# Loading and transposing the columns of the edge products in the relational stage, and comparing fp32 columns into one-hots

## The chip, the cores and the metric

One Trainium2 chip, one core. The metric is the device time of one launch in microseconds (us). The profile is of one execution of the program. Its engines are PE (TensorE matmuls, with PEld for its weight loads), DVE (VectorE), ACT (ScalarE), POOL (GpSimd) and SP (SyncE, which here only issues DMAs; "SPq" in the trace). Each engine works off its own queue in order and waits at semaphores for the others.

## The reference, cut to what matters

A graph network of four layers over 3125 nodes with 256 features each; every layer is a graph part and a feed-forward part, each added to x. There are 53125 edges (src, dst), sorted by dst. What bears on the change:

- layer 1, graph part ("relational"): `agg = segment_sum(hx[edge_type, src], dst)`, where hx holds x times the weight of each of 8 relations
- layer 1, feed-forward part: a mixture of 4 experts, whose gates come from an attention layer over a second list of edges ("the gates")
- layer 2, graph part: two graph convolutions, `segment_sum((h @ W)[src] * norm, dst)`, over the same edges as the relational part

The kernel computes the sums of layer 2 as products with an adjacency matrix in bf16, whose blocks are made in advance. The change is in how these blocks are made.

## The kernel before, in words

Nodes are sorted by degree and cut into 25 groups of 128 (NT = 25); group g has KS[g] edge slots per node (41 for the first, 10 for the last, 453 in all). X, the nodes' rows, stays in SBUF.

**Adjacency blocks.** `edge_places` (L1746) computes for every edge slot the source's partition and a block number and writes both to slots_d in DRAM (L1762, 25 DMAs on SP, at 1692.7 us). `edge_columns` (L1764) reads them back: it fills W ("em_w", 128 x 5 x 2 x 128 fp32) with 512.0 on DVE, loads it with 45 DMAs on SP (L1774, L1777), and makes `columns` ("em_c"), the numbers 0 to 255, by an iota on POOL. The function it returns, `turn` (L1784), transposes W in ten 128x128 transposes on PE into PSUM, from which ACT copies it to `cols` ("em_cols"). `one_hots` (L1793) then compares cols with columns for one group: two tensor_tensor instructions on DVE, into "em_p" (who is the source) and "em_b" (which block). `edge_blocks` (L1804) multiplies the two on PE ("em_ps"), and ACT copies the products to "em_a", which goes to adj in DRAM.

**The relational stage** (from L2253). `plain_sum` (L1690) gathers, slot by slot, 453 tiles of 128 rows from rel with indirect DMAs issued by POOL (L1079), and PE sums them (L1705). `pipeline` (L1088) writes the order of the gathers, sums and tails out by hand (`tc.manual_schedule`) while there are gathers left. Beside it, four steps a turn, runs `route_merge` (L1870), which sorts the second list of edges, mostly on DVE; its first DMA on SP is the load of rm_c (L1890), which PE's L1897 waits for. It uses a PSUM tile m_ps with a single buffer. The tails write gm, the table that the gates gather from.

**The gates** (`gates_by_slots`, L2307) lie inside a `tc.If`. `in_turns` (L1575) writes the order out by hand: turn by turn, for each group, POOL gathers the list (recs, L2327), the node's own row (own, L2329) and 428 tiles from gm (L2334), DVE scores and sums them (L2337 to L2357). Beside it, some pieces a turn, runs `beside_gates` (L2413): 28 units of the experts' hidden layers (L2438, L2452) on PE, and at i = 2 `turn`, from i = 3 on the one-hots of group i - 3, from i = 4 on the products of group i - 4. The first turn takes four pieces, later ones one or two. Once the gates are there, X takes up the experts' rows, which SP loads as y (L2518).

**What is not written out by hand** is put in order by a planner: it takes instructions when it thinks that their inputs and memory are ready, and may place them ahead of others traced earlier. Memory is given out pool by pool; a pool that is opened where another was closed waits for that one's tiles.

Of the kernel before, what the change touches and what calls it, by code (L numbers as in the profile page):

```python
# [11 lines left out]
F32 = mybir.dt.float32  # L12
BF16 = mybir.dt.bfloat16
# [7 lines left out]
P = 128  # L21
# [3 lines left out]
NT = (N + P - 1) // P  # L25
# [1388 lines left out]
def quick(ctx: ExitStack, tc: tile.TileContext, a: dict, out: bass.AP, k):  # L1414
# [3 lines left out]
    nc, dram, ident, ones = tc.nc, k.dram, k.ident, k.ones  # L1418
# [304 lines left out]
    TB = -(-at // P)  # L1723
# [37 lines left out]
            o = slice(OFF[g], OFF[g] + KS[g])  # L1761
            nc.sync.dma_start(slots_of(g).rearrange("(s p k) -> p s k", s=2, p=P), pb[:, :, o])  # L1762

    def edge_columns(wp, psum):  # L1764


        W = wp.tile([P, TB, 2, P], F32, name="em_w")
        nc.vector.memset(W, 512.0)
        for g, (w, n, at) in enumerate(TILES):
            e = w * KS[g]  # L1770
            full, rest = P // w, P % w * KS[g]
            rows = slots_of(g).rearrange("(s m) -> s m", s=2)
            r = at % P
            nc.sync.dma_start(W[r : r + full, at // P, :, :e],  # L1774
                              rows[:, : full * e].rearrange("s (i e) -> i s e", e=e))
            if rest:
                nc.sync.dma_start(W[r + full : r + n, at // P, :, :rest],  # L1777
                                  rows[:, full * e :].rearrange("s (i e) -> i s e", i=1))
        columns = wp.tile([P, 256], BF16, name="em_c")
        nc.gpsimd.iota(columns, pattern=[[1, 256]], base=0, channel_multiplier=0,  # L1780
                       allow_small_or_imprecise_dtypes=True)
        cols = wp.tile([P, TB, 2, P], BF16, name="em_cols")

        def turn():  # L1784
            for b in range(TB):
                ps = psum.tile([P, 2, 256], F32, name="em_ps", bufs=3)
                for s in range(2):
                    nc.tensor.transpose(ps[:, s, :P], W[:, b, s, :], ident)
                nc.scalar.copy(cols[:, b, :, :], ps[:, :, :P])

        return cols, columns, turn

    def one_hots(pool, cols, columns, g):  # L1793
        w, n, at = TILES[g]
        e, z = w * KS[g], w * NT
        part = pool.tile([e, n, P], BF16, name="em_p")
        block = pool.tile([e, n, z], BF16, name="em_b")
        m = slice(at % P, at % P + n)
        for t, s, c in ((part, 0, P), (block, 1, z)):
            nc.vector.tensor_tensor(t, columns[:e, None, :c].to_broadcast([e, n, c]),  # L1800
                                    cols[:e, at // P, s, m][:, :, None].to_broadcast([e, n, c]), ALU.is_equal)
        return part, block
# [182 lines left out]
    with tc.tile_pool(name="gg", bufs=gbufs) as gp, tc.tile_pool(name="gm", bufs=3) as mp, \  # L1985
# [78 lines left out]
        for _ in lists:  # L2064
            pass

    with tc.tile_pool(name="rt", bufs=1) as rt_pool:
        pieces, G = route_pieces(rt_pool)

# [6 lines left out]
        with tc.tile_pool(name="sc", bufs=1) as sc:  # L2076
# [24 lines left out]
            with tc.tile_pool(name="tkp", bufs=1, space=PSUM) as tkp, tc.tile_pool(name="sk", bufs=2) as sk:  # L2101
# [4 lines left out]
                for c0, n in CHUNKS:  # L2106
                    xmt = sk.tile([P, PP, 512], F32, name="xmt")
                    for c in range(PP):
                        ps = tkp.tile([P, 512], F32, name="xm_ps", bufs=2)
# [42 lines left out]
            with tc.tile_pool(name="atp", bufs=1, space=PSUM) as atp, tc.tile_pool(name="sb", bufs=1) as sb:  # L2152
# [18 lines left out]
                for w, nm in ((wq, "qt"), (wk, "kt")):  # L2171
                    ps = atp.tile([P, PP, P], F32, name="a_ps", bufs=3)
# [80 lines left out]
        with tc.tile_pool(name="rg", bufs=12) as gp, tc.tile_pool(name="rs", bufs=2) as sp, \  # L2253
                tc.tile_pool(name="rc", bufs=1) as wp, tc.tile_pool(name="rcp", bufs=1, space=PSUM) as psum:
            wl = f.kxn(a["L1_gnn_loop_weight"], D, wp, "w_loop")
            hb = f.row(a["L1_gnn_h_bias"], D, wp, "h_bias")
            wg = f.kxn(a["L1_ffn_W_gat"], HC, wp, "wg")
            at_r = wp.tile([P, 2, HC], F32, name="at_r")
            for i, n in enumerate(("att_src", "att_dst")):
                ap = a["L1_ffn_" + n]  # L2260
                nc.sync.dma_start(at_r[:, i, :], bass.AP(tensor=ap.tensor, offset=ap.offset, ap=[[0, P], [1, HC]]))

            def loop(acc, g):
                for c in range(KD):
                    nc.tensor.matmul(acc, XNT[:, c, g * P : (g + 1) * P], wl[:, c, :], start=(c == 0), stop=False)

            def tail(g, acc):
                nc.vector.scalar_tensor_tensor(X[:, g, :], acc, 0.5 ** 0.5, X[:, g, :], op0=ALU.mult, op1=ALU.add)
                nc.vector.tensor_add(X[:, g, :], X[:, g, :], hb)
                if g % BATCH < BATCH - 1:  # L2270
                    return
                yield 0
                gs = range(g - BATCH + 1, g + 1)
                yield from norm_pieces(sp, psum, gs)
                tbs = []
                for g_ in gs:
                    ps = psum.tile([P, HC], F32, name="hg_ps", bufs=2)
                    f.node_matmul(ps, g_, wg, slice(0, HC))
                    tb = sp.tile([P, GW], F32, name="tb", bufs=2 * BATCH)
                    tv = tb[:, : H * (C + 1)].rearrange("p (h c) -> p h c", h=H)  # L2280
                    nc.vector.memset(tb, 1.0)
                    nc.vector.tensor_copy(tb.bitcast(I32)[:, H * (C + 3) : H * (C + 3) + 1], place[:, g_ : g_ + 1])
                    nc.scalar.copy(tv[:, :, :C], ps.rearrange("p (h c) -> p h c", h=H))
                    m = sp.tile([P, 2, HC], F32, name="m2")
                    nc.vector.tensor_mul(m, ps[:, None, :].to_broadcast([P, 2, HC]), at_r)
                    nc.vector.tensor_reduce(tb[:, H * (C + 1) : H * (C + 3)],
                                            m.rearrange("p s (h c) -> p (s h) c", h=H), AX.X, ALU.add)
                    tbs.append(tb)
                    yield 0
                yield 0  # L2290
                yield 0
                for g_, tb in zip(gs, tbs):
                    scatter(tc, "gm", gm, pid(g_), tb)
                    yield 0

            merge = route_merge(wp, lambda n: psum.tile([P, P], F32, name="m_ps")[:, :n], pieces, G)
            plain_sum(rel, relz, gp, psum, loop, tail, merge)
            for _ in merge:
                pass


    gd = dram.tile([NP, C], F32, name="gd")
# [110 lines left out]
    def beside_gates(pool, wp, psum):  # L2413
# [6 lines left out]
        ws, hts, os_, ys, hots, As = {}, {}, {}, {}, {}, {}  # L2420
# [43 lines left out]
            nc.sync.dma_start(each_d[e, c0 : c0 + n, :].rearrange("(i p) d -> p i d", p=P), ys.pop(u)[:, : n // P, :])  # L2464

        load(0)
        cols, columns, turn = edge_columns(wp, psum)
        clear = itertools.chain(cleared(sw_in), cleared(top_in))
        U = len(units)
        for i in range(U + 3):  # L2470
            if i % len(CHUNKS) == 2 and i // len(CHUNKS) + 1 < EX:
                load(i // len(CHUNKS) + 1)
            if 0 <= i - 2 < U:
                biased(i - 2)
            if i == 2:
                turn()
            if 3 <= i < NT + 3:
                hots[i - 3] = one_hots(pool, cols, columns, i - 3)
            g = i - 4
            products = iter(())  # L2480
            if 0 <= g < NT:
                As[g] = pool.tile([P, NT, P], BF16, name="em_a")
                products = edge_blocks(psum, g, *hots.pop(g), As[g])
            work = [hidden(i)] if i < U else []
            if 0 <= i - 1 < U:
                work.append(back(i - 1))
            for _ in itertools.chain(*work):
                next(products, None)
            for _ in products:
                pass  # L2490
            if 0 <= i - 3 < U:
                store(i - 3)
            if 0 <= g - 1 < NT:
                nc.sync.dma_start(adj[g - 1], As.pop(g - 1).rearrange("p b j -> p (b j)"))
            next(clear, None)
            yield 0
# [9 lines left out]
    with c2.Else():  # L2506
        with tc.tile_pool(name="gc", bufs=1) as gc:
            gates_by_tiles(gc)
        with tc.tile_pool(name="gc", bufs=1) as gc, tc.tile_pool(name="gx", bufs=2) as xp, \
                tc.tile_pool(name="gxp", bufs=1, space=PSUM) as psum:  # L2510
            for _ in beside_gates(xp, gc, psum):
                pass
    with tc.tile_pool(name="ge", bufs=1) as gc, tc.tile_pool(name="gy", bufs=4) as gp:
        gates = gc.tile([P, NT, C], F32, name="gates")
        nc.sync.dma_start(gates, gd.rearrange("(p t) w -> p t w", p=P))
        for g in range(NT):
            y = gp.tile([P, 4, D], F32, name="y")
            nc.sync.dma_start(y, each_d[:, g * P : (g + 1) * P, :].rearrange("e p d -> p e d"))  # L2518
            for e in range(4):
                nc.vector.scalar_tensor_tensor(X[:, g, :], y[:, e, :], gates[:, g, e : e + 1], X[:, g, :],  # L2520
                                               op0=ALU.mult, op1=ALU.add)
# [476 lines left out]
```

## Time and profile before

| what | us |
|---|---|
| median of 5 runs | 5851.42 |
| lowest and highest run | 5832.91, 5855.75 |
| the profiled execution | 5851.66 |
| its span, from the first to the last instruction | 5849.7 |
| PE busy | 3840.9 (66%) |
| DVE busy | 3125.5 (53%) |
| ACT busy | 1220.0 (21%) |
| POOL busy | 3167.3 (54%) |
| relational stage, in the span | 2102 to 2771 |
| gates, in the span | 2771 to 3513 |
| comparisons L1800, 25 into em_p and 25 into em_b | 69.6 and 89.2 on DVE |

A row of the profile's groups has: line, engine, operation, output and inputs by the program's names, count; busy time in us and the mean of one in ns; the idle time of the engine ahead of them, and what ended it. A line in order of time has: start in the span, duration, engine, line, operation, and in brackets the idle time ahead of it with what ended it ("issue" where it waited for nothing that the profile shows). The table by stage has for each engine the busy time and the number of instructions, then the granted TensorE clock, the share of the DMA engines and their rate.

### The profile page before, as it was taken

The numbers are of one execution on the slowest core, as the hardware profiler recorded it, in microseconds if no ns is written. First come the engines' busy times: TensorE is split into PE (matmuls) and PEld (weight loads), VectorE is DVE, ScalarE is ACT, GpSimd is POOL, SyncE is SP. The second block draws the span as 40 slices with busy tenths as digits, with TensorE's granted clock in tenths as the row PEclk, the third lists the DMA queues.
The fourth block names the chain that finished last, engine by engine and source line by source line (L and its number), as shares of the span: only waits on it lengthen the run. The fifth ranks groups of instructions, "written<-read, shape, count | busy, mean of one in ns | idle before, by whom it ended". The sixth has DMA issues, their size and how long they took to land. (4 is left out here: it accounts for less than half of the span.)

```text
span 5849.7 us, 45124 instructions
## 1 busy us (share of the span) xinstructions
PE 3840.9 (66%) x14119; PEld 2472.2 (42%) x14119; DVE 3125.5 (53%) x6023; ACT 1220.0 (21%) x2574; POOL 3167.3 (54%) x3044
## 2 busy tenths in 40 slices
PE   2345544355578978676866602989587999658882
PEld 1234333233455534344544401556343555446661
DVE  4588877999975356611444416332226889700001
ACT  1222222445642200000333301110021000012220
POOL 4577774777776057777777773010106777520005
PEclk9676766667789976666988856999656878779996
DMA  4533343333321233323532214332243333334442
GB/s 123 147 105 108 107 109 87 100 97 102 108 51 46 111 101 105 101 73 88 152 109 64 67 31 146 105 106 96 75 129 94 102 99 100 104 124 158 151 158 83
DMA packets 357952, 602.93 MB, mean 103 GB/s; under 512 B 109331, under 2 KB 254331, under 8 KB 354370
## 3 DMA queue, kind: packets, MB, share of 16 engines
q0 software_dynamic: 130800, 329.16, 20.9%
q1 hardware_dynamic: 207657, 251.79, 13.4%
q10 hardware_dynamic: 19238, 18.93, 1.0%
q8 instruction: 115, 1.88, 0.1%
q14 instruction: 142, 1.16, 0.1%
HBM read 458.77 MB, written 142.93 MB: 103 GB/s over the span
## 5 line engine op out<-in xcount | busy, mean ns | idle before, releaser
L1620 PE MATMUL acc<-wv,ident 128*128 128x256 f32 x2818 | 906.6, 481 | 574.4 <-ACT wv L1632 296.2
L1079 POOL DMA_INDIRECT gt<-T,recs x906 | 1005.1, 1109 | 307.9 <-issue 219.6
L1620 PEld LDWEIGHTS acc<-wv,ident 128*128 128x128 f32 x2818 | 652.4, 242 | 828.6 <-ACT wv L1632 343.9
L1079 POOL DMA_INDIRECT gt<-gm,recs x428 | 511.4, 1195 | 138.9 <-issue 115.5
L1079 POOL DMA_INDIRECT gt<-TA,recs x453 | 469.4, 1036 | 139.4 <-issue 122.8
L1079 POOL DMA_INDIRECT gt<-rel,relz x453 | 441.3, 974 | 141.8 <-issue 121.5
L1705 PE MATMUL acc<-gt,ident 128*128 128x256 f32 x906 | 419.2, 577 | 144.0 <-DMA gt<-rel,relz 136.9
L2566 PE MATMUL acc<-XNT,adj_g 128*128 128x512 bf16 x1250 | 416.2, 384 | 47.0 <-ACT XNT L2558 47.0
L1672 ACT ACTIVATE m<-m 128x1024 f32<-128x1024 f32 (+2 forms) x258 | 256.5, 994 | 625.5 <-DVE m L1671 625.2
L1079 POOL DMA_INDIRECT y<-top_out,top_pos x50 | 47.8, 957 | 596.9 <-issue 595.7
L1671 DVE TENSOR_TENSOR m<-gt,R 128x1028 f32<-128x1028 f32 (+4 forms) x258 | 297.4, 1153 | 117.9 <-DMA gt<-T,recs 114.5
L1705 PEld LDWEIGHTS acc<-gt,ident 128*128 128x128 f32 x906 | 202.8, 264 | 342.8 <-DMA gt<-rel,relz 330.6
L2569 PE MATMUL acc<-F,adj_g 128*128 128x256 bf16 x1250 | 342.9, 275 | 5.7 <-DVE F L2559 5.7
L2438 PE MATMUL x_ps<-XNT,x_w 128*128 128x512 f32 (+1 forms) x448 | 214.8, 613 | 172.1 <-ACT x_h L2440 161.9
L2797 PE MATMUL e_ps<-EW,att 32*128 32x512 f32 (+7 forms) x466 | 289.7, 747 | 49.8 <-ACT att L2787 33.7
L2909 PE MATMUL fh_ps<-xt,w 128*128 128x256 f32 x1024 | 266.9, 399 | 76.2 <-ACT ht L2911 75.4
L1677 DVE TENSOR_TENSOR m<-m,att 128x1024 f32<-128x1024 f32 (+2 forms) x258 | 294.2, 1140 | 27.8 <-ACT m L1672 27.8
L1678 DVE TENSOR_REDUCE L<-m 128x4 f32<-128x1024 f32 (+4 forms) x258 | 294.3, 1141 | 8.0
L1634 DVE TENSOR_TENSOR wv<-gt,L 128x1024 f32<-128x1024 f32 (+3 forms) x252 | 285.3, 1137 | 0.9 <-PE acc L1620 0.8
L2909 PEld LDWEIGHTS fh_ps<-xt,w 128*128 128x128 f32 x1024 | 187.7, 193 | 150.3 <-ACT ht L2911 128.1
L2901 DVE COPY xt<-ft_ps 128x512 f32<-128x512 f32 x32 | 22.1, 692 | 388.9 <-PE ft_ps L2900 388.9
L1083 POOL DMA_INDIRECT gcn<-own,PR x50 | 64.6, 1291 | 304.4 <-ACT ht L1455 228.5
(557 smaller groups left out, 6748.4 us busy)
## 6 DMA issues: line engine op xcount, KB each, us to landing
w<-in_L_ffn_W_dram SPq DMA_DIRECT2D x64, 1024.0 KB
adj_g<-adj SPq DMA_DIRECT2D x50, 800.0 KB
adj<-em_a SPq DMA_DIRECT2D x25, 800.0 KB
gt<-T,recs POOLq DMA_INDIRECT x906, 2.8
y<-each_d SPq DMA_DIRECT2D x25, 512.0 KB
each_d<-x_y SPq DMA_DIRECT2D x24, 512.0 KB
R<-rr SPq DMA_DIRECT2D x25, 388.0 KB
top_in<-zeros SPq DMA_DIRECT2D x8, 1024.0 KB
```

The source lines that it names most:

```text
L1079: return nc.gpsimd.indirect_dma_start(out=out_, out_offset=None, in_=table, in_offset=index(idx))
L1620: nc.tensor.matmul(acc, ident, wv[:, s, :], start=(c + s == 0), stop=(c + s == K - 1))
L1634: nc.vector.tensor_mul(wv[:, :n, :].rearrange("p s (h c) -> p s h c", h=H), t[:, :n, :D].rearrange("p s (h c) -> p s h c", h=H), L[:, c : ...
L1671: nc.vector.tensor_add(m[:, :n, :], st[g].tiles[c][:, :n, :], st[g].R[:, 1:2, :].to_broadcast([P, n, W]))
L1672: nc.scalar.activation(m[:, :n, :D], m[:, :n, :D], AF.Abs)
L1677: nc.vector.tensor_mul(m[:, :n, :D], m[:, :n, :D], att[:, None, :].to_broadcast([P, n, D]))
L1678: nc.vector.tensor_reduce(L, m[:, :n, :D].rearrange("p s (h c) -> p s h c", h=H), AX.X, ALU.add)
L1705: nc.tensor.matmul(accs[g], ident, t[:, s, :], start=False, stop=(last and s == n - 1))
L2566: nc.tensor.matmul(acc.rearrange("p s d -> p (s d)"), A[:, b, :], F12[:, b, :, :].rearrange("p s d -> p (s d)"), start=(b == 0), stop=Fals ...
L2569: nc.tensor.matmul(acc[:, 0, :], A[:, b, :], F3_[:, b, :], start=False, stop=(b == NT - 1), skip_group_check=True)
L2797: nc.tensor.matmul(e_ps[:, :z, :].rearrange("p s d -> p (s d)"), att, EW[: att.shape[0], s0 : s0 + z, :].rearrange("p s d -> p (s d)"), st ...
L2909: nc.tensor.matmul(ps[:, i, :], ld[j][1][:, c, (f_ + i) * P : (f_ + i + 1) * P], xt[j][:, c, :], start=(c == 0), stop=(c == KD - 1))
```

## The change

`edge_columns` takes a pool for W, and is called before `plain_sum` in the relational stage instead of at the start of `beside_gates`. The call hands eq over as wp: columns and cols lie in the new pool "eq", which is opened ahead of the slice attention (`held`) and closed after the gates; W lies in the pool that is handed over as `pool`, the relational stage's own. `turn` is called after the merge, at the end of the relational stage, goes through the m_ps tile one transpose at a time, and makes ten copies instead of five. columns and cols are fp32 instead of bf16, so that both inputs of the comparisons in `one_hots` are fp32; their outputs remain bf16. In `beside_gates` the one-hots of group i are made at i, and the products of group i - 1 at i: three pieces earlier than before.

```diff
-    def edge_columns(wp, psum):
+    def edge_columns(wp, pool):
-        W = wp.tile([P, TB, 2, P], F32, name="em_w")
+        W = pool.tile([P, TB, 2, P], F32, name="em_w")
         nc.vector.memset(W, 512.0)
...
-        columns = wp.tile([P, 256], BF16, name="em_c")
+        columns = wp.tile([P, 256], F32, name="em_c")
         nc.gpsimd.iota(columns, pattern=[[1, 256]], base=0, channel_multiplier=0,
                        allow_small_or_imprecise_dtypes=True)
-        cols = wp.tile([P, TB, 2, P], BF16, name="em_cols")
-
-        def turn():
+        cols = wp.tile([P, TB, 2, P], F32, name="em_cols")
+
+        def turn(psum):
             for b in range(TB):
-                ps = psum.tile([P, 2, 256], F32, name="em_ps", bufs=3)
                 for s in range(2):
-                    nc.tensor.transpose(ps[:, s, :P], W[:, b, s, :], ident)
-                nc.scalar.copy(cols[:, b, :, :], ps[:, :, :P])
+                    ps = psum.tile([P, P], F32, name="m_ps")
+                    nc.tensor.transpose(ps, W[:, b, s, :], ident)
+                    nc.scalar.copy(cols[:, b, s, :], ps)
...
+    held = ExitStack()
+    eq = held.enter_context(tc.tile_pool(name="eq", bufs=1))
     with tc.tile_pool(name="rt", bufs=1) as rt_pool:
...
+            cols, columns, turn = edge_columns(eq, wp)
             merge = route_merge(wp, lambda n: psum.tile([P, P], F32, name="m_ps")[:, :n], pieces, G)
             plain_sum(rel, relz, gp, psum, loop, tail, merge)
             for _ in merge:
                 pass
+            turn(psum)
...
         load(0)
-        cols, columns, turn = edge_columns(wp, psum)
...
-            if i == 2:
-                turn()
-            if 3 <= i < NT + 3:
-                hots[i - 3] = one_hots(pool, cols, columns, i - 3)
-            g = i - 4
+            if i < NT:
+                hots[i] = one_hots(pool, cols, columns, i)
+            g = i - 1
...
+    held.close()
```

## The prediction

> **What bounds the kernel now.** I read the slices of the span first, then the groups, then the order in time around the places that the diff touches. The change lies in two stages: the relational one (2102 to 2771 us of the span) and the gates (2771 to 3513). The table by stage shows neither PE nor DVE full there:
>
> ```profile
> core 0: us, PE busy (x) PEld busy (x) DVE busy (x) ACT busy (x) POOL busy (x), PEclk, DMA share, GB/s
> 2102.00:2771.00 669.00, 477.76 (x1164) 264.29 (x1164) 302.43 (x723) 14.59 (x55) 504.53 (x543) 0.65 0.34 91
> 2771.00:3513.00 742.00, 434.58 (x1751) 279.69 (x1751) 283.77 (x492) 224.95 (x476) 581.63 (x501) 0.79 0.32 85
> ```
>
> POOL is the bound of both. In the gates it has 501 instructions, 0.30 us pass between two of them ("issue"), and 581.6 + 501 x 0.30 = 732 of the 742 us. So what the change is worth is what it does to POOL's queue. Of that queue one row is too dear:
>
> ```profile
> L1079 POOL DMA_INDIRECT gt<-gm,recs x428 | 511.4, 1195 | 138.9 <-issue 115.5
> ```
>
> Undisturbed such a gather takes 0.94 us. Laid beside DVE in order of time, it is seen what stretches the others:
>
> ```profile
> 2817.20 5.88 DVE L1800 TENSOR_TENSOR em_p<-em_c,em_cols 123x5504 bf16<-123x5504 bf16 x1
> 2818.00 5.90 POOL L1079 DMA_INDIRECT gt<-gm,recs  x1 [0.98 <-DMA gt<-gm,recs]
> 2823.00 3.52 DVE L1800 TENSOR_TENSOR em_b<-em_c,em_cols 123x3225 bf16<-123x3225 bf16 x1
> 2824.21 3.12 POOL L1079 DMA_INDIRECT gt<-gm,recs  x1 [0.30 <-issue]
> ```
>
> The first gather ends at 2823.90, 0.82 us after em_p ends (2823.08); the second at 2827.33, 0.81 after em_b. I went through the whole stage: of the 51 gathers that start under an L1800, 50 are stretched, and the mean of the 51 is 3.08 us. That is 51 x (3.08 - 0.94) = 109 us of POOL's time. The question of the change is therefore whether an fp32 comparison holds POOL for less.
>
> **fp32 comparisons.** The same two views in the relational stage answer it. L1926 is a tensor_tensor of fp32 with both inputs in SBUF:
>
> ```profile
> 2134.99 2.29 DVE L1926 TENSOR_TENSOR rp_g<-rp_g,rm_t 125x2048 f32<-125x2048 f32 x1
> 2136.09 2.02 POOL L1079 DMA_INDIRECT gt<-rel,relz  x1 [0.30 <-issue]
> ```
>
> This gather ends at 2138.11, 0.83 after the fp32 instruction: held in the same way. So are gathers under L1671, L1677 and L1634 of the attention layers (f32, 45 stretched in 300 us, nearly all ending 0.81 to 0.84 us after it). And the length: an em_p of 128x2048 bf16 takes 2.30 us, L1926 with 2048 fp32 elements 2.29, L1924 with int32 against f32 2.29. Fp32 inputs with a bf16 output are not in the trace; the nearest rows bound the difference by 0.02 us either way, x 50 instructions = -1 to +1 us. I take 0, as the rows are equal.
>
> The Trainium skill speaks against this edit: "VectorE: DVE Perf Modes", section "The perf-mode tier table", gives tensor_tensor twice the rate on bf16 in SBUF that it has on fp32. By that the 158.8 us of comparisons would double, and an estimate from that page is up to 159 us more on POOL, some 6010 us. This trace disagrees: its bf16 comparisons run at the fp32 rate already, and one of their inputs is broadcast along the inner axis, where the page asks for a step of one. On the hold, the skill's "SBUF - State Buffer", section "Who interferes with whom", infers that a tensor_tensor doesn't starve the making of descriptors; the 50 rows above differ, and the measurement decides.
>
> **The columns leave the gates.** What goes, one by one. On POOL the iota em_c (0.37 us, 0.28 before the next): it stands between the gather of own and the first of gt, on the path: -0.65. On DVE the memset (1.12 us): DVE then idles 27.8 us until PE's first output, 0. On PE 10 transposes (1.55 us) and on ACT 5 copies (1.55): neither is the bound, 0. On SP 45 loads, 2774.2 to 2799.9, 25.7 us; queued behind them are zeros for sw_in and the second expert's weights, issued at 2801 and used an expert later: 0.
>
> **Where they go.** columns and cols lie in the new pool eq, W in the relational stage's own pool, whose memory comes free at 2102 us. So the 45 loads can't be moved into SP's idle time before (it issues nothing from 1849.3 to 2102.3); only the em_c iota can. The start of the stage, in order of time:
>
> ```profile
> 2102.29 0.37 SPq L57 DMA_DIRECT2D w_loop<-n_L_gnn_loop_weight_dram  x1
> ...
> 2104.68 0.43 SPq L1890 DMA_DIRECT2D rm_c<-route_n  x1
> 2110.70 0.42 PE L1897 MATMUL m_ps<-rm_c,ones 128*128 128x2 f32 x2
> 2112.94 0.15 DVE L1900 COPY rm_b<-m_ps 128x2 f32<-128x2 f32 x1
> 2113.20 2.81 DVE L1909 TENSOR_SCALAR rm_t<-rp_g 125x2048 int32<-125x2048 int32 x1
> ...
> 2118.77 2.29 DVE L1914 TENSOR_TENSOR rm_t<-rm_t,rm_u 125x2048 int32<-125x2048 int32 x1
> 2130.36 2.28 POOL L1915 IOTA rm_u<- 125x2048 int32 x1
> 2132.67 2.29 DVE L1924 TENSOR_TENSOR rm_t<-rm_u,rm_n 125x2048 f32<-125x2048 int32 x1 [6.88 <-POOL rm_u L1915]
> ```
>
> The reader is to see a chain: rm_c, a small sum on PE, four passes on DVE, then POOL's second iota into rm_u, which must wait until L1914 has read the first. It has 9.3 us of slack (2121.06 to 2130.36).
>
> W's memset and loads are traced ahead of plain_sum, and rm_c stands inside the order written by hand, behind them. What the planner did with work of that kind: the zero rows of rel (L2073), traced after two attention layers, go out at 184.7 us; the iota of place (L2252) stands at 1669.5, ahead of 128 gathers traced before it. It goes by readiness, then by traced order. The loads are ready once the memset is done (1.1 us after 2102), so I put them ahead of rm_c. Then, step by step: five other loads as now, 45 loads by the 25.7 us that they took in the gates, rm_c issued at 2104.7 + 25.7 = 2130.4. A small load of this place lands some 2.5 us after its issue (h_bias issued at 2102.71, first read on PE at 2105.2), so L1897 runs at about 2133 and L1900 at 2133.5. It then takes L1909 (2.81, of which 1.6 look like POOL's first iota beside it: the like L1912 takes 1.23), L1910 1.29, L1912 1.23, L1914 2.29: it ends between 2140.0 and 2141.5. POOL waits from 2130.4 to there: 9.6 to 11.1 us more. Two gathers that now run before the iota, undisturbed, come to lie under these passes: about 1.8 us. Together 11.4 to 12.9, and I take the middle: **+12.2 us**.
>
> What of the rest of the 20 us by which DVE is late? DVE waits 34.8 us for POOL's rm_base (L1953, 2487.7) and 8.5 for rm_all (L1933): there the merge catches up. PE's sums start late by as much, but 12 chunk buffers lie between, and POOL nowhere waits for PE beyond its 0.30. Nothing further is late: 0. What would speak against it is in the third rival. On POOL the iota em_c, hoisted, falls among early gathers with idle time behind them (21 us before 2069.7): 0.
>
> **The transposes.** Ten rounds through a single m_ps buffer: transpose, copy, transpose. The nearest row is the norm's round (two transposes and a copy of 128x256), 1.17 us a round at the end of this stage, so at most 12 us on PE and ACT. m_ps is free from 2627, when the merge ends. PE idles 191 us of this stage and is buffered by 12 chunks; ACT works 15 us of 669. Put last instead, the rounds fall into PE's wait of 10.2 us for the first weights (2767.3 to 2777.5): at worst 2 us, on PE, which isn't the bound. I take 0.
>
> **One-hots and products three pieces earlier.** The same 25 pairs, still within POOL's gathers, hold POOL as long as before: 0 (-1 to +1 for how they meet the gathers). New is that the first turn holds four pairs instead of one. Could DVE then be late for POOL? The gathers of group 4 need the tile that group 0's sum frees: that sum ends at 2874, they start at 2958.9, 85 us of margin. PE's extra is three products of about 3.0 us (74.5/25), less the 1.55 of transposes. 0.
>
> **Sum.** The profiled execution took 5851.66 us (span 5849.7 and 2.0 around it). 5851.66 - 0.65 + 12.2 = 5863.2; the median of the runs, 5851.42, lies 0.2 lower. I forecast 5863. Its own range takes POOL's wait and the stretched gathers from below and above, with 3 to 5 us for what the steps at nothing may bring: 5858 to 5871.
>
> **Rivals.**
> 1. *Not slower: rm_c goes ahead of the loads.* If the planner or the hand-written order takes rm_c first, or the loads are spread between the steps of the merge, the chain stands as it is and only the iota's 0.65 is left: 5851. It decides while rm_c is issued before about 2119 (L1914 ends 9.6 to 11.1 us after rm_c's issue in the steps above, and POOL wants it read at 2130.4). For it: readiness alone (rm_c needs nothing but memory, the loads a memset first). Against it: rm_c is traced inside the hand-ordered part, behind the loads.
> 2. *Faster: rm_c ahead, and transfers around the gates earlier.* POOL's waits in the gates beyond 0.30 us add up to some 10.8 us (2.07, 0.81, 4.04, 1.04, 1.34 and smaller), mostly for lists whose transfers are late; without 45 loads ahead of them they might go, and the loads of y (1.84 us each) start one sooner in eq's memory. 5851.0 - 10.8 - 1.8 = 5838. Against it: the bulk transfers of weights remain, only 25.7 us sooner.
> 3. *Slower by the whole delay.* rm_c is late by 25.7 us, of which 19.6 to 20.6 reach L1914; if the later waits of POOL for the merge grow too (5.1 us for L1217 at 2509.7 is one), POOL loses all of it: 5851 + 20 = 5871. Against it: the 34.8 us that DVE waits for POOL shortly before.
> 4. *fp32 does release POOL.* Then 109 us go: 5742 without a delay. Against it stand the L1926 rows.
> 5. *fp32 costs DVE more.* Each per cent of the 158.8 us holds POOL 1.6 us longer: ten per cent and the delay make 5879. Against it: the equal lengths.
>
> **How the numbers follow.** Forecast 62%, first rival 20, second 8, third 8, fourth 1, fifth 1. The bound of 0.2% is 11.7 us here (about what a measurement of this kernel can tell from no change), so slower begins at 5863.1, in the middle of the forecast's own range; of its 13 us, 8 lie above, so I count 37 of its 62 as slower and 25 as the same. Slower: 37 + 8 + 1 = 46%. The same: 25 + 20 = 45%. Faster: 8 + 1 = 9%. The range takes in the forecast and the first three rivals at their prices, and leaves out the last two: 5838 to 5872.
>
> **What would show it.** Right: em_w's loads on SP from about 2104 to 2130 and rm_c behind them; POOL waiting ahead of rm_u's second iota until about 2140; no iota of em_c in the gates; L1800's groups with f32 inputs at the lengths of now (2.3 us for 128x2048) and gathers of gm at a mean near 1195 ns. Wrong: rm_c near 2105 (first and second rival), a longer wait of POOL near 2510 (third), a mean of gm near 0.95 us (fourth), longer L1800 (fifth), or a wait of POOL for DVE early in the gates, which would say that the 85 us of margin were not there.

## The result, and the profile after

The changed kernel takes 5847.81 us (median of 34 runs, 5831.29 to 5865.35), the kernel before 5851.07 (58 runs): a ratio of 0.9996, 95% interval 0.9990 to 1.0002. That is no change. The profiled execution of the changed kernel took 5851.69 us, with a span of 5849.9, the same as before.

A difference of nothing hides two stages that moved by 8 us and more. First the relational stage, in order of time, after the change:

```profile
2125.46 1.82 POOL L2737 MEMSET EW<- 32x2048 f32 x1
2128.39 0.35 SPq L1890 DMA_DIRECT2D rm_c<-route_n  x1
2135.35 2.29 DVE L1914 TENSOR_TENSOR rm_t<-rm_t,rm_u 125x2048 int32<-125x2048 int32 x1
2137.71 3.22 POOL L1915 IOTA rm_u<- 125x2048 int32 x1 [10.43 <-DVE rm_t L1914]
```

The 45 loads of em_w stand on SP from 2104.55 to 2128.28, rm_c behind them: 23.7 us later than before. L1914 ends at 2137.64 instead of 2121.06, and POOL, which before reached its second iota with no wait, now idles 10.43 us ahead of it. One line is new here, and no part of the diff speaks of it: EW, the table of edge weights of the last layer, is filled on POOL at 2125. It is not alone: the five other loads of its pool on SP (w, bias, wg, bg, a_row), issued from 3408.7 on before, now go out right behind rm_c, from 2128.8 on.

The other place is the end of the gates. Before the change (first fence) EW's fill and its 16 loads on SP stood between the last scatter of the gates and the load of `gates`; after it (second fence) they are gone from there:

```profile
3532.32 0.96 POOL L1083 DMA_INDIRECT gd<-gates_o,own_at  x1 [0.30 <-issue]
3533.28 1.82 POOL L2735 MEMSET EW<- 32x2048 f32 x1
...
3540.26 0.35 SPq L2515 DMA_DIRECT2D gates<-gd  x1
```

```profile
3537.03 0.97 POOL L1083 DMA_INDIRECT gd<-gates_o,own_at  x1 [0.30 <-issue]
3539.21 0.34 SPq L2517 DMA_DIRECT2D gates<-gd  x1
```

From the start of the last scatter to the load of `gates` it was 7.9 us and is 2.2.

I followed POOL's gathers one by one through both traces, and noted how much later each starts after the change. The list is the account of the whole result:

| place | later than before by, us |
|---|---|
| gather 20 of rel (2140.9 before) | 9.3 |
| last gather of rel | 8.1 |
| first gather of gm | 8.2 |
| gather 20 of gm | 23.6 |
| gather 200 of gm | 15.5 |
| last gather of gm | 4.7 |
| load of `gates` | -1.1 |
| end of the last sum of the experts' rows into X | 2.2 |
| span | 0.2 |

The first row adds up from single differences: the first gather +0.65; gathers ahead of the iota, which no longer lie under the merge's passes, -5.5; EW's fill +1.8; the wait +10.4; the iota, now beside a pass of DVE, +0.9; gathers after it +1.0. A later wait of POOL for DVE (L1217) became 1.2 us shorter. In the gates the four pairs of comparisons of the first turn now hold the first gathers (+15.4 by gather 20), and later gathers are freed in return, until the gates have taken 3.5 us less than before (737.2 to 733.7 from the first gather to the last): 2.2 of them on the gathers of lists, one of which lay under a comparison before, and 1.1 on those of gm. The last 5.7 are EW. Behind the load of `gates` that gain doesn't stay whole: the 25 loads of y take 48.0 us from the first to the last where they took 45.6, so the last sum into X ends 2.2 us later than before. Why they take longer isn't known. From there to the end the changed kernel is 2.0 us quicker, which is little beside the 34 us over which the runs of one kernel are spread.

The comparisons themselves have not changed. This is the last one into em_p, before (first fence) and after:

```profile
3359.50 1.88 DVE L1800 TENSOR_TENSOR em_p<-em_c,em_cols 100x1664 bf16<-100x1664 bf16 x1
```

```profile
3307.24 1.88 DVE L1800 TENSOR_TENSOR em_p<-em_c,em_cols 100x1664 bf16<-100x1664 f32 x1
```

The group of gathers from gm takes 510.3 us (511.4 before), and under the comparisons 50 gathers are still stretched:

```profile
L1079 POOL DMA_INDIRECT gt<-gm,recs x428 | 510.3, 1192 | 139.0 <-issue 116.7
```

### The profile page after: what moved, and what is told of

It reads as the page before. It is cut to its first block, busy times and chain, and to the rows that moved or that the text cites. A ratio compares the mean times of both kernels' runs of the same rounds, so it can differ in the third digit from the quotient of the medians.

```text
span 5849.9 us, 45128 instructions
## 1 busy us (share of the span) xinstructions
PE 3839.9 (66%) x14119; PEld 2475.5 (42%) x14119; DVE 3125.7 (53%) x6023; ACT 1221.6 (21%) x2579; POOL 3156.5 (54%) x3044
## 5 line engine op out<-in xcount | busy, mean ns | idle before, releaser
L1079 POOL DMA_INDIRECT gt<-gm,recs x428 | 510.3, 1192 | 139.0 <-issue 116.7
L2923 PE MATMUL fo_ps<-w,ht 128*128 128x256 f32 x1024 | 226.3, 379 | 0.0
```

Source lines behind the costliest of these rows:

```text
L1079: return nc.gpsimd.indirect_dma_start(out=out_, out_offset=None, in_=table, in_offset=index(idx))
L2923: nc.tensor.matmul(ps[:, i, :], h[:, f_, i * P : (i + 1) * P], w2[:, f_, :], start=(f_ == 0), stop=(f_ == FC3 - 1))
```

## The experiments

Theory T, formed from the account above: the edits act through POOL's queue; the late rm_c costs 8 to 9 us, EW's new place brings nearly 6 ahead of the load of `gates`, the shorter gates the rest, and the element type nothing. Its main rival, U: what happens on POOL in the relational stage is absorbed later anyway, so that neither of the first two has a price. Runs on two of the three chips used can't settle a few us: there the kernel before takes 6296 us (chip of a_late, a_pad, a_bf16, a_psum) and 6222 us (b_fp32, a_sched, a_psum_late, a_both), with intervals of 0.3%. On the chip of a_late2, a_pad2, a_psum2 and a_flat it takes 5851.45.

**1. rm_c ahead of the loads.**

```diff
-            cols, columns, turn = edge_columns(eq, wp)
             merge = route_merge(...)
             plain_sum(rel, relz, gp, psum, loop, tail, merge)
             for _ in merge:
                 pass
+            cols, columns, turn = edge_columns(eq, wp)
             turn(psum)
```

> The changed kernel with the memset and the 45 loads of em_w traced after the merge, so that SP issues rm_c ahead of them; nothing else moves. Theory T (POOL's queue carries the delay to the end): POOL's wait of 10.43 us ahead of rm_u's second iota goes, the first gather of gm starts 8 us earlier than in the changed kernel (near 2775 instead of 2783), and the time falls from 5847.8 to about 5840 (5836 to 5843). Rival U (the end of the gates isn't set by POOL, the delay is absorbed anyway): the wait goes too, but the time stays at 5848 (5845 to 5851).

> The same kernel again (rm_c issued ahead of em_w's loads), because the first run fell on a chip on which the kernel before took 6296 us, where 8 us can't be told. Theory T: POOL's wait ahead of rm_u's second iota goes and the whole program ends 8 us sooner than the changed kernel: a ratio to the kernel before of 0.9982 (0.9975 to 0.9990), on a chip with the time of the first result near 5840. Rival U: the wait goes and the ratio stays at 0.9996 (0.9990 to 1.0002).

The planner leaves the loads in the relational stage and only moves rm_c ahead of them; the order of PE, ACT and POOL is that of the changed kernel, and on DVE em_w's memset alone goes two places back. Chip of 6296 us: a ratio of 1.0000 (0.9967 to 1.0033), which tells nothing. Chip of 5851 us: 5839.8 us, 0.9978 (0.9969 to 0.9987). In its trace, in order of time:

```profile
2102.89 0.43 SPq L1890 DMA_DIRECT2D rm_c<-route_n  x1
2116.96 2.29 DVE L1914 TENSOR_TENSOR rm_t<-rm_t,rm_u 125x2048 int32<-125x2048 int32 x1
2128.55 1.82 POOL L2737 MEMSET EW<- 32x2048 f32 x1
2130.30 2.27 POOL L1915 IOTA rm_u<- 125x2048 int32 x1
```

POOL's wait is gone. The first gather of gm starts 9.1 us earlier than in the changed kernel and the last 9.3 earlier: nothing absorbs it up to there. T holds, and U falls for this term, since 0.9996 lies outside the interval. This kernel is also 0.2% faster than the kernel before, with one line moved. Its gates take 733.5 us from the first gather to the last, as in the changed kernel (733.7), so it isn't the delay that made them shorter.

**2. EW back at its old place.** An unused tile takes the memory in the gates' pool that em_w and em_cols left.

```diff
         load(0)
+        hold_ = wp.tile([P, TB, 3, P], F32, name="em_pad")
+        nc.vector.memset(hold_, 512.0)
         clear = itertools.chain(cleared(sw_in), cleared(top_in))
```

> The changed kernel with an unused tile of 7.5 KB per partition (and its memset on DVE) in the gates' pool, where em_w and em_cols lay before the change; it occupies the memory by which EW (the edge weights of the last layer) came to be filled in the relational stage. Theory T: EW's memset and 16 loads return to the place behind the gates' last scatter, 5.8 us between that scatter and the load of the gates come back, of which the loads of y give back some 1 to 3: 5851 to 5854. Rival U (what stands between the gates and the sums of the experts' rows is absorbed): 5848, unchanged to 2 us.

> The same kernel again (EW's fill returned to the place behind the gates' last scatter). Theory T: a ratio to the kernel before of 1.0004 to 1.0010 (5851 to 5855). Rival U: 0.9996 as without the tile (5848).

Chip of 6296 us: 1.0028 (0.9994 to 1.0062). Chip of 5851 us: 5853.4 us, 1.0006 (0.9997 to 1.0015), the middle of what T expects; the interval overlaps with that of the changed kernel, so the time alone doesn't refute U. The trace shows the mechanism:

```profile
3536.83 0.96 POOL L1083 DMA_INDIRECT gd<-gates_o,own_at  x1 [0.30 <-issue]
3537.79 1.82 POOL L2739 MEMSET EW<- 32x2048 f32 x1
...
3544.44 0.36 SPq L2519 DMA_DIRECT2D gates<-gd  x1
```

7.6 us again from the last scatter's start to the load of `gates`. POOL's wait ahead of rm_u's second iota is 12.14 us here, 1.7 more than with EW's fill in front of it: in the changed kernel the fill stood where POOL would have waited anyway, and cost nothing. The five other loads of its pool are back as well, at 3413.5. So it is shown that the memory that em_w and em_cols left decides where EW is filled, and that this is worth 5.4 (here) to 5.7 us at the load of `gates`. How far it carries, the traces show in part. From the start of the last scatter to the end of the last sum of the experts' rows, the kernels with EW's fill in the relational stage take 59.0, 58.4 and 58.4 us (the changed kernel, a_late2 and a_psum2 of experiment 5), those with it behind the gates 63.6 and 63.8 (a_pad2 and a_flat of experiment 5): 4.6 to 5.4 us. The kernel before takes 61.5 there, its loads of y being quicker, so that between it and the changed kernel 2.5 us are left. That the gain is in the total time is probable, not shown.

**3. The element type.** In a_bf16 the changed kernel has bf16 columns, in b_fp32 the kernel before has fp32 ones (two words of `edge_columns` each); no engine's order differs from the kernel that each was made from.

> The changed kernel with columns and cols in bf16 as before, nothing else. Theory T (the element type costs nothing): comparisons of the same length (2.30 us for 128x2048), gathers of gm at a mean of 1.19 us, 5848 (5845 to 5851). Rival V (fp32 inputs halve the rate, by the perf-mode rule): comparisons near half, some 75 us less on DVE, and POOL held that much less: near 5770.

> The kernel before with columns and cols in fp32 and nothing else changed: the dtype part alone; the order of every engine's instructions is that of before. Theory T: ratio 1.0000 (0.9993 to 1.0007), comparisons of 128x2048 at 2.29 to 2.31 us. Rival V (fp32 costs the comparisons part of their rate): each per cent is 1.6 us, so from 7% on the ratio would be over 1.002.

Ratios to before: 1.0004 (0.9974 to 1.0034) and 1.0002 (0.9968 to 1.0035). The lengths say it better than these times: 1.881 us for the shortest em_p and 3.484 and 3.483 for the shortest em_b, in both. V falls. (The mean of the gathers of gm, 1.11 us in a_bf16 where T had 1.19, is that of a chip on which POOL waits for more and fewer gathers meet a comparison.)

**4. The places of the one-hots and products.** The edit takes the diff's last part back: one-hots of group i - 3 and products of group i - 4 at i.

> The changed kernel with the one-hots and products at their places of before (three and four pieces later), everything else as changed. Theory T: the same 25 pairs hold POOL equally, so the gates take as long: ratio to before 0.9993 to 1.0001 (the changed kernel: 0.9996); the first 20 gathers of gm lose the 15 us by which they were later, and gathers after 3300 us of the span get them back. Rival Y (the earlier place is what made the gates 3.5 us shorter in the changed kernel): 3 to 4 us more, 1.0002.

0.9998 (0.9972 to 1.0023) on the chip of 6222 us: no effect as large as 0.3%. It can't tell T from Y, which lie 0.01 to 0.09% apart. Open.

**5. What holds POOL.** Two kernels measure the hold itself. In a_flat the comparison is read from one dense tile, without a broadcast. In a_psum ACT copies columns into PSUM once:

```diff
+        cp = psum.tile([P, 256], F32, name="em_cp")
+        nc.scalar.copy(cp, columns)
...
-                hots[i] = one_hots(pool, cols, columns, i)
+                hots[i] = one_hots(pool, cols, cp, i)
...
-                ps = psum.tile([P, 2, 256], F32, name="em_ps", bufs=3)
+                ps = psum.tile([P, 2, 256], F32, name="em_ps", bufs=2)
```

> Leaves out the true comparison: both inputs of L1800 are read from one constant bf16 tile, with a step of one and no broadcast, so the one-hots are wrong; it measures rate and hold alone (and its tile of 11 KB puts EW's fill behind the gates, as in a_pad). If a broadcast input is what keeps bf16 at the fp32 rate: 128x2048 takes about 1.2 us instead of 2.30, and DVE's 159 us become about 80. If bf16 tensor_tensor has no faster rate at all here: 2.30 us. If the hold goes by the instruction's end, gathers end 0.82 us after these too, and those that start under them take about 1.5 to 2 us instead of 3.

> The changed kernel with columns copied once into PSUM by ACT and compared from there (one buffer less for em_ps, 2 instead of 3). Theory T (a DVE instruction with both inputs in SBUF holds POOL's descriptor work until 0.82 us after its end, one with an input in PSUM doesn't): gathers of gm at a mean of 0.95 to 1.0 us instead of 1.19, 510 us of them becoming 405 to 430, and a time of 5740 to 5765. Rival W (every long DVE instruction holds POOL): the mean stays at 1.19, 5848 to 5860. Rival X (PE or DVE becomes the bound of the gates once POOL is faster): the mean falls, but POOL waits, 5770 to 5830.

> The same kernel again (columns compared from PSUM). On the slow chip the gathers of gm had a mean of 0.946 us, and POOL then waited 302 us in all beside them, much of it for DVE's L2346: rival X there. Theory T now: the mean is 0.95 us again; where transfers are as quick as in the first profile, POOL's waits in the gates stay below 50 us and the time is 5740 to 5790. Rival X (PE and the pieces beside the gates are then the bound, whatever the chip): POOL's waits take the gain, 5820 to 5900.

a_flat, one execution: 5780.33 us. In order of time, near the start of the gates:

```profile
2786.49 1.84 DVE L1800 TENSOR_TENSOR em_b<-em_wide 123x3225 bf16<-123x3225 bf16 x1
2787.69 1.44 POOL L1079 DMA_INDIRECT gt<-gm,recs  x1 [0.30 <-issue]
2788.23 1.88 DVE L1800 TENSOR_TENSOR em_p<-em_wide 125x3328 bf16<-125x3328 bf16 x1
2789.44 1.50 POOL L1079 DMA_INDIRECT gt<-gm,recs  x1 [0.30 <-issue]
```

3225 elements take 1.84 us where they took 3.52: dense bf16 inputs get a faster rate, the broadcast ones of this kernel don't. (The longest comparison went from 5.94 in the changed kernel to 3.03, all 50 from 158.7 us to 83.3. The edit takes away both broadcasts and reads both inputs from one tile; which of these matters wasn't tried alone.) The first gather ends at 2789.13, 0.80 us after em_b: POOL is held all the same, for a shorter time.

a_psum2, on the same chip: 5752.93 us, 0.9833 (0.9821 to 0.9846). In order of time at the same place, and its group:

```profile
2788.36 3.51 DVE L1800 TENSOR_TENSOR em_b<-em_cp,em_cols 123x3225 bf16<-123x3225 f32 x1
2790.25 0.94 POOL L1079 DMA_INDIRECT gt<-gm,recs  x1 [0.30 <-issue]
2791.50 0.94 POOL L1079 DMA_INDIRECT gt<-gm,recs  x1 [0.30 <-issue]
2791.78 3.62 DVE L1800 TENSOR_TENSOR em_p<-em_cp,em_cols 125x3328 bf16<-125x3328 f32 x1
2792.74 0.95 POOL L1079 DMA_INDIRECT gt<-gm,recs  x1 [0.30 <-issue]
```

```profile
L1079 POOL DMA_INDIRECT gt<-gm,recs x428 | 406.5, 950 | 145.2 <-issue 115.9
```

The comparisons are as long as with fp32 in SBUF, yet gathers pass under them at 0.94 us. Of 119 gathers that start under a comparison (those of lists and own rows counted in) one is stretched; in the changed kernel it was 50 of 52. The 104 us less of POOL's time become 95 us from the first gather to the last (733.7 to 638.6), and 98 us against the kernel before: W falls. On this chip X falls too.

**6. The same on another chip, and both edits together.** a_psum_late is a_psum once more; a_both adds experiment 1 to it.

> A second timing of the comparisons from PSUM, on the chip of the next one. Theory T: ratio 0.983 as before (0.982 to 0.985).

> Both edits on top of the changed kernel: rm_c ahead of em_w's loads, and columns compared from PSUM. Theory T (both act on POOL's queue, one in each stage, so they add): 98 us less from the second and 9 to 11 from the first, a ratio to before of 0.9815 (0.9800 to 0.9830), about 5743. Rival Z (once POOL is faster, PE or the transfers of the experts set the end of the gates, and the first stage's 9 us are waited away): 0.983, as with PSUM alone.

On the chip of 6296 us a_psum takes 6394.4 us, 1.0189 (1.0145 to 1.0233); on that of 6222 us a_psum_late takes 1.0221 (1.0185 to 1.0257) and a_both 1.0208 (1.0173 to 1.0244). So what is 1.7% faster on one chip is 2% slower on two others. The gathers are as short there (of the 140 that start under a comparison in these three runs none is stretched), and POOL waits; the group of a_psum_late:

```profile
L1079 POOL DMA_INDIRECT gt<-gm,recs x428 | 405.7, 948 | 298.2 <-DVE pen L2346 164.4
```

The loss lies in the gates: from the first gather to the last they take 970 us in a_psum and 855 in a_late on the same chip. Among the products beside the gates there are stretches like this one, in the middle of the first turn, in order of time (ACT and PE alone):

```profile
3012.74 0.28 ACT L1817 CAST em_a<-em_ps 128x150 bf16<-128x150 f32 x1 [5.32 <-remote]
3013.08 0.29 PE L1813 MATMUL em_ps<-em_b,em_p 123*128 123x75 bf16 x2 [5.31 <-ACT em_a L1817]
3018.34 0.29 ACT L1817 CAST em_a<-em_ps 128x150 bf16<-128x150 f32 x1 [5.32 <-remote]
3018.68 0.28 PE L1813 MATMUL em_ps<-em_b,em_p 123*128 123x75 bf16 x2 [5.32 <-ACT em_a L1817]
```

PE and ACT take turns, one round in 5.60 us, though each works 0.3 us of it; on the other chip 14 such copies run in 4.10 us. Rival X has the waits right on these chips: POOL ends up waiting for DVE. But X still counted on a gain, and why the kernel becomes slower than the kernel before isn't shown. The rounds alone don't account for it: on the chip of 6296 us a_late, a_pad and a_bf16, with three buffers, have 11, 14 and 10 rounds of 5.5 to 5.7 us, a_psum has 11, and the first three are not measurably slower than the kernel before. On the chip of 6222 us a_psum_late has 13 and a_both 9, while b_fp32 and a_sched, whose one-hots stand at the places of before, have none. Whether the buffer that em_ps gave up (2 instead of 3) causes the loss, or the earlier gathers do, was not tried. Whether the two gains add (T) or not (Z) is open: on this chip the relational stage of a_both is 7.5 us shorter than that of a_psum_late (763.0 to 770.5), its gates are 11 us longer, and the intervals overlap.

## Why the prediction was right or wrong

The forecast was 5863 and the range 5838 to 5872; the time is 5848. Step by step:

- *The loads stay ahead of rm_c (the likeliest case).* Right: readiness, then traced order. rm_c was issued at 2128.4 (forecast 2130.4), since 45 loads took 23.7 us and not 25.7. L1914 ended 2.4 us ahead of the lower end that was forecast: 2.0 of them are the shorter loads, the rest the quicker way from rm_c to L1900 (2.7 us after rm_c's issue, 3.1 forecast). L1909 took 1.22 us without the iota beside it, as that lower end already had it.
- *POOL waits 9.6 to 11.1 us.* Measured 10.43, partly by luck: L1914 was 2.4 us or more earlier than forecast, but POOL came 3.1 us earlier too (2127.3 for 2130.4), EW's fill of 1.8 us included.
- *Stretched gathers, +1.8.* Wrong in sign. The passes moved away from gathers that they had stretched (-5.5) and fell on POOL's own wait, where they hold nothing; what came back later was 1.0, and 0.9 on the iota. The step looked at the two gathers that would come under the passes and not at the five that would leave them. (The third rival's 19.6 to 20.6 us should by its own steps be 18.9 to 20.4; its price of 20 stands.)
- *Nothing further is late.* Right: the delay stayed between 7.8 and 9.3 us through the stage, and the wait at the perm scatters became shorter, not longer.
- *fp32 at 0.* Right (experiment 3): broadcast bf16 already ran at the fp32 rate, and a_flat shows the dense bf16 rate that it didn't have. The Trainium skill, "VectorE: DVE Perf Modes", section "The perf-mode tier table", has the faster bf16 rate; these runs show it for dense inputs (1.84 against 3.52 us) and not for the broadcast ones of this kernel.
- *Iota, transposes, products: 0 to -0.65.* POOL's delay doesn't grow while the transposes run (2640 to 2669). The gates became 3.5 us shorter where the forecast had 0 with 1 us either way; it named the mechanism ("how they meet the gathers") and gave it too little room. Which part of the edit did it is open (experiment 4).
- *What failed: the sum holds no term for memory.* The prediction weighed the edit's instructions and the queues they pass, and of memory only where em_w would lie and, in the second rival, where y would. It did not ask who would lie where em_w and em_cols had lain. EW did, and 5.7 us ahead of the load of `gates` went away, a term that the sum put at nothing.

So of +11.5 forecast, +8.2 was there when the gates began, and 3.5 and 5.7 that were not priced had taken it back by the load of `gates`. That the time lies within the range is therefore luck: the range reached down to 5838 for two rivals in which rm_c goes first, and rm_c did not. The first rival's time (5851) came out, but not its mechanism. That the total moved by nothing says nothing about the parts, as experiment 1 shows.

## What to carry to other kernels

When a tile is moved to another pool, look for what the planner will put into the place that it leaves, and whether that stood on a path: here a fill for a much later layer was worth 5.7 us at the place that it left, beside a wait of 10.4 that the change added. When a group of loads is moved into a stage, put the one load that a chain waits for ahead of them (9 us for one line). And where POOL's indirect DMAs are the bound, look at DVE's operands before its element types: one input in PSUM freed 104 us of POOL's time on which fp32 or bf16 alone had no effect; but time such a gain on more than one chip.

## What the runs showed of the hardware

- The comparisons (tensor_tensor) with both inputs in SBUF hold the gathers until 0.81 to 0.84 us after their end, with bf16 inputs, with fp32 ones, broadcast, or dense at the faster rate (140 of the 144 stretched gathers of the kernel before, the changed kernel and a_flat); with one input in PSUM, 118 of 119 gathers under them in a_psum2 were not held, at the same length on DVE (3.51 us for 123x3225).
- Three chips gave 5851, 6222 and 6296 us for the same kernel. The two slower ones show a granted clock of 0.76 where the other shows 0.78, and in some of the kernels stretches in which a hand-over between PE and ACT takes some 5 us. What brings these about isn't known.
